# Combining the early deformable samples inside the attention and storing only their combination

## The chip, the cores and the metric

The program runs on one core of a Trainium2 chip. A core has five engines that run side by side, each with its own in-order stream of instructions: TensorE (PE, with its weight loads PEld), VectorE (DVE), ScalarE (ACT), GpSimd (POOL) and SyncE (SP). They tell each other by semaphores when a tile is ready or free. DMAs are issued from the streams of SP, POOL and ACT and run on 16 DMA engines. SBUF is the on-chip memory with 128 partitions, PSUM the small accumulator memory that PE writes. The metric is the device time of one execution in microseconds (us); the median of several runs is given.

## The reference, cut to what matters

The input has two images of 256 channels and 64 x 64 pixels, all in fp32. Four layers follow each other:

1. group norm, attention with 4 heads over all 4096 pixels, projection, residual;
2. a position term is added;
3. a bottleneck: 1x1 convolution to 64 channels, a modulated deformable 3x3 convolution, 1x1 convolution back, residual;
4. two deformable 3x3 convolutions over 256 channels, each after a group norm and a ReLU, and a residual.

The deformable convolution of layer 4 samples the image at nine displaced positions per pixel, each from four neighbours:

```python
y0, x0 = jnp.floor(py), jnp.floor(px)
wy1, wx1 = py - y0, px - x0
out = (gather(y0, x0) * (wy0 * wx0) + gather(y0, x0 + 1) * (wy0 * wx1)
     + gather(y0 + 1, x0) * (wy1 * wx0) + gather(y0 + 1, x0 + 1) * (wy1 * wx1))
...
out = jnp.einsum('bckhw,ock->bohw', sampled, w.reshape(O, C, KK))
```

With separate weights for the two axes, the left pair of neighbours (both rows) can be scaled by wx0, the right pair scaled by wx1 and added, and the two rows of the result then weighted by wy0 and wy1.

## The kernel before, in words

**Two phases.** `attention` computes layer 1 for both images, and in the gaps of its loop the bottleneck of image 0 and the preparation of layer 4 for image 0. `deform` then computes the four deformable convolutions (two images, two layers) and, in the gaps of its first part, the bottleneck of image 1. The order of PE, ACT, DVE and POOL is the order in which the program emits the instructions; SP's is placed by the framework.

**The attention loop.** It runs over score tiles n of 128 queries by 1024 keys, 256 for each of four units (image, pair of heads), two tiles per turn of the loop; such a turn is called a pair here. A pair evicts the transposes of tile n-1, computes the scores of n+2 and n+3 on PE (L583), their row maxima on DVE (`lowest`, L595) and exponentials on ACT (`exponentials`, L601), transposes the exponentials of n and n+1 on PE (`turn`, L613), copies the transposes out of PSUM (`keep`, L630 on DVE and L632 on ACT) and multiplies those of an earlier tile with the values (`attend`, L642). A finished product is copied by DVE (L474). Steps with a due time (`own`) and background generators (`back`) are worked off at fixed places of the pair: `small(n)`, `small(n + 1)` and `background`. Among the due steps are the sharing of the softmax sums through DRAM (`spread`: SP stores shares, waits, and loads f), the weighting on POOL (`combine`, L522 to L530, at steps that are multiples of 16 plus 4) and the projection (`project`, L547).

**The early samples.** In the last unit the generator `early_samples` works out, for the first EARLY = 5 blocks of 512 pixels of image 0, where to sample (`offsets`, `corners`), and puts 36 samples per block in a queue: nine taps times four groups of 128 pixels, 180 samples in all. `self.sample()` is called at the end of every pair, twice, or once where n % 16 == 4. A call can store one gathered sample to DRAM and gather one: the gather (L858, POOL) fetches for each of 128 pixels one row of `img3`, which holds upper and lower neighbour side by side, and its right neighbour: 4 x 256 values per pixel, 512 KB. The store (L1299, POOL) writes these 512 KB to `samp_d`. Three tiles hold samples under way, five once the last block's offsets are done.

**The deformable phase.** It runs over samples s: 36 per block of 512 pixels, 8 blocks per layer. Per step it issues a gather for s+8, `left(s + 3)` on ACT (L1510: the left half times its weight), `right(s + 2)` on DVE (L1516: the right half times its weight, added), `first` on ACT (L1525) and `others` on DVE (L1529 or L1535) for the two rows, transposes on PE (L1547), an eviction on ACT (L1556) and products on PE (L1566). For the 180 early samples the gather is replaced by a load from `samp_d` (L1487), the first eight issued by POOL and the others by SP. Ten tiles hold samples. In these first steps the generator `second` runs the bottleneck of image 1 (`conv`): 288 gathers on POOL (L858), weighting and adding on DVE (L1077, L1088), transposes and products on PE (L1113, L1125, L1147) that share one PSUM bank, evicted by ACT (L1117).

Of the kernel before, what the change touches and what calls it, by code (L numbers as in the profile page):

```python
# [11 lines left out]
F32 = mybir.dt.float32  # L12
# [8 lines left out]
P = 128  # L21
# [3 lines left out]
CM = 64  # L25
# [39 lines left out]
class Net:  # L65
    def __init__(self, ctx, tc, a, out):
        self.tc, self.nc, self.a, self.out = tc, tc.nc, a, out
        nc = self.nc
        const = ctx.enter_context(tc.tile_pool(name="const", bufs=1))
        self.small = ctx.enter_context(tc.tile_pool(name="small", bufs=2))  # L70
        dram = ctx.enter_context(tc.tile_pool(name="dram", bufs=1, space=DRAM))

        self.ident = const.tile([P, P], F32, name="ident")
        make_identity(nc, self.ident)
        self.vec = const.tile([P, V_COLS], F32, name="vec")
        nc.sync.dma_start(self.vec, a["vec"])
        self.sel = const.tile([P, 32], F32, name="sel")
        self.shift = const.tile([P, DWK, 32], F32, name="shift")
        self.later = [(self.sel, a["sel"]), (self.shift, a["shift"])]

        self.img2, self.img3, self.x2d = [], [], []

        self.xn_d, self.xa_d = [], []
        for b in range(B):
            self.img2.append(dram.tile([GH * GW, 2 * CM], F32, name=f"img2_{b}"))
            self.img3.append(dram.tile([GH * GW, 2 * C], F32, name=f"img3_{b}"))
            self.x2d.append(dram.tile([C, HW], F32, name=f"x2d_{b}"))
            self.xn_d.append(dram.tile([C, HW], F32, name=f"xn_{b}"))
            self.xa_d.append(dram.tile([C, HW], F32, name=f"xa_{b}"))

        self.pos_d = dram.tile([C, HW], F32, name="pos_d")

        self.samp_d = [dram.tile([4 * K2 * P, 4 * C], F32, name=f"samp_d{i}") for i in range(EARLY)]
        self.sample = lambda: False
        self.early = {}
        self.share_d = [dram.tile([16, P], F32, name=f"share_d{n}") for n in range(2)]

        vec = self.vec
        self.bn_s = const.tile([P, 4], F32, name="bn_s")
        self.bn_t = const.tile([P, 4], F32, name="bn_t")  # L100
# [80 lines left out]
    def attention(self, bott):  # L181
# [5 lines left out]
        with ExitStack() as ctx:  # L187
# [492 lines left out]
            while n < last + 4 or back or more or any(own.values()):  # L680
                u, d = divmod(n, per_unit)
                if d == 0 and u < len(units):
                    plan_unit(u)
                    if u == 0:
                        back.append(prepare(1))
                    if u == 1:
                        back.append(bott.before(0, bt, ps))
                    if u == 2:
                        back.append(first_batch())
                    if u == 3:  # L690
                        back.insert(0, bott.before(1, bt, ps))
                        back.append(self.early_samples(bott, bt, held, xp, vp, kp, ps))

                def small(at):
                    steps = own.pop(at, ())
                    for f in steps:
                        f()
                    if not steps and u > 1:
                        background(1)

                if n - 1 in pts:
                    p = pts.pop(n - 1)
                    keep(n - 1, p, "ACT")
# [12 lines left out]

                small(n)
                if 4 <= n < last + 4:
                    attend(n - 4)
                    attend(n - 3)  # L720
                small(n + 1)
                if n < last:
                    pts[n + 1] = turn(e.pop(n + 1))
                if sc:
                    e[n + 3] = exponentials(n + 3, sc[1])
                if u or n % 8 == 0:
                    background(1 + (u > 1 and n % 4 == 0))

                for _ in range(2 - (n % 16 == 4)):
                    more = self.sample()  # L730
                n += 2


# [522 lines left out]
    def early_samples(self, bott, pools, held, xp, vp, kp, ps):  # L1256
# [32 lines left out]
            self.filters(wf[cb], cb, dw, pw)  # L1289
            yield True  # L1290
        free, more = deque(x.rearrange("p u n -> p (u n)") for x in xbs), [border, t]
        gathers, stores = deque(), deque()

        def gather():


            if len(stores) > 1 and len(free) < 3 or not gathers and stores:
                dst, four = stores.popleft()
                nc.gpsimd.dma_start(dst, four)  # L1299
                free.append(four)  # L1300
            if gathers:
                dst, idx = gathers.popleft()
                four = free.popleft()
                self.gather(four, self.img3[0], idx)
                stores.append((dst, four))
            return gathers or stores

        self.sample = gather
        for i in range(EARLY):
            idx = bott.corner.tile([P, 4, K2], I32, name="bidx")  # L1310
            w = bott.corner.tile([P, 4, K2, 4], F32, name="bw4").rearrange("p a k c -> p (a k c)")
            w = self.early[i] = w.rearrange("p (s j k t) -> p s j k t", s=2, j=4, t=2)
            steps = self.offsets(
                i, xs,
                lambda s, row: wf[s][:, DWK * row : DWK * row + DWK, :].rearrange(
                    "p t o -> p (t o)"
                ),
                self.vec[:, V_PWB : V_PWB + 1],
                bott.base, idx, None, pools["work"], wide, ps,
                odp=lambda: pools["t"].tile([P, 512], F32, name="bst"), y0=rows(i)[0],  # L1320
                later=ps.later, w=w,
            )
            mine = False
            for done in steps:
                if done == "bank":
                    continue
                while bott.lock and not mine:
                    yield False
                bott.lock = mine = True
                yield True  # L1330
            bott.lock = False
            if i + 1 < EARLY:
                load(i + 1)
            if i + 1 == EARLY:
                free.extend(more)
            for m in range(4 * K2):
                k, j = divmod(m, 4)
                gathers.append((self.samp_d[i][m * P : m * P + P, :], idx[:, j, k : k + 1]))

    def deform(self, bott):  # L1340

# [4 lines left out]
        with ExitStack() as ctx:  # L1346
# [130 lines left out]
            def gather(s):  # L1477
                if s < ALL:
# [4 lines left out]
                    if n == 0 and i < EARLY:  # L1483

                        queue = nc.gpsimd if s < AHEAD else nc.sync
                        m = 4 * k + j
                        queue.dma_start(four, self.samp_d[i][m * P : m * P + P, :])  # L1487
                        return
                    idx = corners[b, l, i][0]
                    self.gather(four, self.img3[b], idx[:, j, k : k + 1])  # L1490
# [6 lines left out]
            def paired(s):  # L1497
                n, i, _, j = parts(s)
                return s < ALL and (n == 0 or j % 2 == 1)

            def share(s, side, axis):
                n, i, k, j = parts(s)
                w = corners[(*layers[n], i)][2]
                return w[:, side, j, k, axis : axis + 1]

            def left(s):

                if paired(s):
                    uv = fours[s][:, 0:2].rearrange("p s c -> p (s c)")
                    nc.scalar.mul(uv, uv, share(s, 0, 1))  # L1510

            def right(s):
                if paired(s):
                    four = fours[s].rearrange("p s c -> p (s c)")
                    uv = four[:, : 2 * C]
                    nc.vector.scalar_tensor_tensor(  # L1516
# [263 lines left out]
```

## Time and profile before

| what | value |
|---|---|
| median of 3 runs | 5226.75 us (5212.4 to 5232.05) |
| profiled execution | 5197.2 us |
| its span, first to last instruction | 5195.3 us |
| PE busy | 4853.1 us (93%) |
| DVE busy | 3970.8 us (76%) |
| ACT busy | 3283.0 us (63%) |
| POOL busy | 2448.6 us (47%) |
| mean granted TensorE clock | 0.975 |
| DMA, whole execution | 1113.50 MB, mean 214 GB/s |
| samples of the early blocks stored, each 512 KB | L1299, 2416.2 to 3062.1 us |
| samples loaded back, each 512 KB | L1487, 3083.7 to 3590.8 us |

How to read it: the engines run side by side, so busy shares do not add up, and a mean over the whole execution says little about a stage. Matmuls are pipelined and their ends are modelled, so a busy PE is not PE at its peak. In a group or timeline line, the engine and line of the kernel come first, then operation, output tile, input tiles and shapes; what stands in brackets or behind the second bar is the idle time of that engine just before, with what ended it ("issue" where the profile shows no reason). Line numbers are those of the kernel before.

### The profile page before, as it was taken

What the parts mean: (1) busy time and instruction counts of PE and PEld (TensorE: products, weight loads), DVE (VectorE), ACT (ScalarE), POOL (GpSimd) and SP (SyncE); (2) the same over time, 40 slices, a digit from 0 to 9 for tenths busy, and PEclk for the clock granted to TensorE, in tenths of its full rate; (3) what the DMA queues carried; (4) which work ended last, traced back from release to release, by engine and by line L of the source; (5) the groups of instructions that cost most, each with busy time, mean ns of one, the idle gap of its engine ahead of it and who ended that gap; (6) DMA issues with size and microseconds to landing.
All of it is one profiled execution on the core that took longest, in us unless ns stands there. A gap on an engine that the chain in (4) does not pass through costs nothing.

```text
span 5195.3 us, 101328 instructions
## 1 busy us (share of the span) xinstructions
PE 4853.1 (93%) x38680; PEld 2726.4 (52%) x38680; DVE 3970.8 (76%) x7081; ACT 3283.0 (63%) x5941; POOL 2448.6 (47%) x2436
## 2 busy tenths in 40 slices
PE   8999999999999999999999976788999999999998
PEld 5555565555555555555555544444444444444443
DVE  6878767878668878765577657787778888888887
ACT  5676656666566666654566655556866766666665
POOL 0111111111117888721455557774766666666665
PEclk9999999999999999999999988889999999999999
DMA  4221111111112333326799988887989999999998
GB/s 169 64 95 52 47 56 48 42 38 38 54 56 87 117 99 111 109 89 213 261 348 355 353 327 294 293 305 283 347 326 329 367 350 352 347 394 351 354 355 299
DMA packets 398998, 1113.50 MB, mean 214 GB/s; under 512 B 65053, under 2 KB 102491, under 8 KB 398511
## 3 DMA queue, kind: packets, MB, share of 16 engines
q0 software_dynamic: 222480, 784.79, 41.7%
q1 hardware_dynamic: 175486, 322.11, 18.7%
q8 instruction: 303, 4.96, 0.4%
q14 instruction: 185, 1.51, 0.1%
q10 hardware_dynamic: 544, 0.13, 0.0%
HBM read 914.48 MB, written 183.97 MB: 211 GB/s over the span
## 4 chain that ended last, share of the span: by engine, by line
PE 27%; DMA 9%; DVE 8%; issue 5%; ACT 3%; POOL 2%; another core or an unknown queue 2%; SPq 0%; DVEq 0%; ACTq 0%; POOLq 0%
PE out L1566 12%; PE pd L815 5%; PE pt L1547 3%; DMA samp_d<-bx 2%; DVE smp L1535 2%; DMA samp_d<-xb 2%; DVE four L1516 2%; DMA four<-img,didx 2%; DVE smp L1529 1%; PE av L642 1%; DMA xb<-img,bidx 1%; PE sc L583 1%; PE pm L815 1%; DMA bx<-img,bidx 1%
## 5 line engine op out<-in xcount | busy, mean ns | idle before, releaser
L601 ACT ACTIVATE e<-sc,low 128x1024 f32<-128x1024 f32 x1024 | 1147.2, 1120 | 755.5 <-DVE low L595 715.1
L595 DVE TENSOR_REDUCE low<-sc 128x1 f32<-128x1024 f32 x1024 | 1204.6, 1217 | 272.3 <-PE sc L583 259.9
L858 POOL DMA_INDIRECT four<-img,didx x972 | 1033.9, 1064 | 582.6 <-issue 223.0
L1566 PE MATMUL out<-st,wc 128*128 128x512 f32 x2304 | 1223.3, 613 | 88.2 <-ACT st L1556 48.0
L583 PE MATMUL sc<-k,qs 64*128 64x512 f32 x2048 | 1003.7, 609 | 0.3 <-DVE k L368 0.3
L642 PE MATMUL av<-et,v 128*64 128x256 f32 x8192 | 998.1, 386 | 0.7 <-DVE et L630 0.7
L583 PE MATMUL sc<-k,q 64*128 64x512 f32 x2048 | 985.9, 608 | 0.0
L613 PEld LDWEIGHTS tt<-ident,e 64*128 64x128 f32 x16384 | 652.1, 139 | 552.1 <-issue 266.9
L632 ACT COPY et<-tt 128x512 f32<-128x512 f32 x1152 | 659.4, 585 | 205.3 <-PE tt L613 161.3
L613 PE MATMUL tt<-ident,e 64*128 64x64 f32 x16384 | 727.7, 227 | 60.8 <-ACT et L632 36.2
L630 DVE COPY et<-tt 128x512 f32<-128x512 f32 x896 | 611.9, 683 | 172.8 <-PE tt L613 164.5
L642 PEld LDWEIGHTS av<-et,v 128*64 128x64 f32 x8192 | 553.9, 137 | 308.7 <-issue 56.6
L858 POOL DMA_INDIRECT bfour<-img,bidx x576 | 611.4, 1062 | 208.8 <-issue 107.3
L1535 DVE SCALAR_TENSOR_TENSOR smp<-four,dw,smp 128x256 f32<-128x256 f32 x1296 | 625.9, 483 | 57.6 <-issue 20.8
L1547 PEld LDWEIGHTS pt<-ident,smp 128*128 128x128 f32 x2304 | 328.7, 143 | 650.1 <-issue 532.5
L522 POOL TENSOR_TENSOR o<-o,f 128x1024 f32<-128x1024 f32 x48 | 113.9, 2373 | 1086.7 <-DVE o L474 540.0
L1566 PEld LDWEIGHTS out<-st,wc 128*128 128x128 f32 x2304 | 385.2, 195 | 325.6 <-issue 212.9
L1516 DVE SCALAR_TENSOR_TENSOR four<-four,dwt 128x512 f32<-128x512 f32 x540 | 403.7, 748 | 155.7 <-ACT four L1510 116.0
L1547 PE MATMUL pt<-ident,smp 128*128 128x128 f32 x2304 | 447.9, 277 | 22.0 <-DVE smp L1529 17.2
L1510 ACT ACTIVATE four<-four,dwt 128x512 f32<-128x512 f32 x540 | 388.1, 719 | 125.1 <-DMA four<-img,didx 105.6
L583 PEld LDWEIGHTS sc<-k,qs 64*128 64x128 f32 x2048 | 348.0, 189 | 214.0 <-issue 125.8
L1556 ACT COPY st<-pt 128x1024 f32<-128x1024 f32 x288 | 289.5, 1005 | 252.1 <-PE pt L1547 175.3
(201 smaller groups left out, 5411.8 us busy)
## 6 DMA issues: line engine op xcount, KB each, us to landing
four<-samp_d SPq DMA_DIRECT2D x172, 512.0 KB
samp_d<-xb POOLq DMA_DIRECT2D x118, 512.0 KB
f<-share_d SPq DMA_DIRECT2D x128, 256.0 KB
xb<-xn SPq DMA_DIRECT2D x55, 512.0 KB
img<-imgt SPq DMA_DIRECT2D x96, 256.0 KB
xa<-res SPq DMA_DIRECT2D x32, 512.0 KB
samp_d<-k POOLq DMA_DIRECT2D x31, 512.0 KB
samp_d<-bx POOLq DMA_DIRECT2D x31, 512.0 KB
```

The source lines that it names most:

```text
L583: nc.tensor.matmul(s[:, j, :], lhsT=q[u, i // 2][int(h != j)][halves[j], at : at + P], rhs=k[u][c][halves[j], h, :], start=True, stop=True,)
L595: nc.vector.tensor_reduce(low, s, AX.X, ALU.max, negate=True)
L601: nc.scalar.activation(e.rearrange("p j n -> p (j n)"), s, AF.Exp, bias=blk.low[:, g, c : c + 1], accum_out=blk.sum[:, g, c : c + 1],)
L613: nc.tensor.transpose(pt[:, m, :], e[half, m // 4, m % 4 * P : m % 4 * P + P], self.ident[half, half],)
L630: nc.vector.tensor_copy(dst, pt)
L632: nc.scalar.copy(dst, pt)
L642: nc.tensor.matmul(now["av"][halves[h], :], lhsT=v[u][c][:, m, halves[h]], rhs=ets[j][:, m, h, :], start=(m == 0), stop=(m == 7),)
L858: self.nc.gpsimd.indirect_dma_start(out=dst, out_offset=None, in_=img, in_offset=bass.IndirectOffsetOnAxis(ap=idx, axis=0),)
L1516: nc.vector.scalar_tensor_tensor(uv, four[:, 2 * C :], share(s, 1, 1), uv, ALU.mult, ALU.add)
L1535: nc.vector.scalar_tensor_tensor(smps[s], four[:, c], weight(s, c), smps[s], ALU.mult, ALU.add)
L1547: nc.tensor.transpose(pts[u][:, c, j * P : (j + 1) * P], smp[:, c * P : c * P + P], self.ident,)
L1566: nc.tensor.matmul(outs[ob], lhsT=wc[k][:, c, ob * P : ob * P + P], rhs=sts[u][:, c, :], start=(k == 0 and c == 0), stop=(k == K2 - 1 and ...
```

## The change

The left and right halves of an early sample are combined in the attention, and only the combination, 2 x 256 values per pixel or 256 KB, is stored. `sample` becomes a line of four stations, one step each per call: SP stores a finished combination; DVE adds the weighted right half (and frees the gathered tile); ACT scales the left half of a gathered sample into a tile of the bottleneck's pool "g" (five buffers); POOL gathers the next sample. ACT takes a sample only when all tiles but one hold gathered samples, or when there is nothing left to gather. One of the two calls per pair moves from the end of the pair to behind `small(n)`, before the products. In the deformable phase the load fetches 256 KB, and `left` and `right` skip the early samples (`whole`); `first` and `others` do what they did.

```diff
-        self.samp_d = [dram.tile([4 * K2 * P, 4 * C], F32, name=f"samp_d{i}") for i in range(EARLY)]
+        self.samp_d = [dram.tile([4 * K2 * P, 2 * C], F32, name=f"samp_d{i}") for i in range(EARLY)]
...
                 small(n)
+                if n % 16 != 4:
+                    self.sample()
                 if 4 <= n < last + 4:
...
-                for _ in range(2 - (n % 16 == 4)):
-                    more = self.sample()
+                more = self.sample()
                 n += 2
...
-        gathers, stores = deque(), deque()
-
-        def gather():
-
-
-            if len(stores) > 1 and len(free) < 3 or not gathers and stores:
-                dst, four = stores.popleft()
-                nc.gpsimd.dma_start(dst, four)
+        gathers, landing, scaled, stores = deque(), deque(), deque(), deque()
+        tiles = len(free)
+
+        def sample():
+
+            if stores:
+                nc.sync.dma_start(*stores.popleft())
+            if scaled:
+                dst, four, uv, w = scaled.popleft()
+                nc.vector.scalar_tensor_tensor(
+                    uv, four[:, 2 * C :], w[:, 1], uv, ALU.mult, ALU.add
+                )
                 free.append(four)
-            if gathers:
-                dst, idx = gathers.popleft()
+                stores.append((dst, uv))
+            if len(landing) >= tiles - 1 or not gathers and landing:
+                dst, four, w = landing.popleft()
+                uv = pools["g"].tile([P, 2, 4, CM], F32, name="bfour")
+                uv = uv.rearrange("p k s c -> p (k s c)")
+                nc.scalar.mul(uv, four[:, : 2 * C], w[:, 0])
+                scaled.append((dst, four, uv, w))
+            if gathers and free:
+                dst, idx, w = gathers.popleft()
                 four = free.popleft()
                 self.gather(four, self.img3[0], idx)
-                stores.append((dst, four))
-            return gathers or stores
+                landing.append((dst, four, w))
+            return gathers or landing or scaled or stores
...
             if i + 1 == EARLY:
                 free.extend(more)
+                tiles += len(more)
...
-                        queue.dma_start(four, self.samp_d[i][m * P : m * P + P, :])
+                        queue.dma_start(four[:, : 2 * C], self.samp_d[i][m * P : m * P + P, :])
...
+            def whole(s):
+                n, i, _, _ = parts(s)
+                return paired(s) and (n > 0 or i >= EARLY)
...
             def left(s):
 
-                if paired(s):
+                if whole(s):
...
             def right(s):
-                if paired(s):
+                if whole(s):
```

More of the change, by code (lines that the diff above doesn't have):

```diff
@@ L1291, in early_samples @@
         free, more = deque(x.rearrange("p u n -> p (u n)") for x in xbs), [border, t]
-        gathers, stores = deque(), deque()
-        def gather():
-            if len(stores) > 1 and len(free) < 3 or not gathers and stores:
-                dst, four = stores.popleft()
-                nc.gpsimd.dma_start(dst, four)
-                free.append(four)
-            if gathers:
-                dst, idx = gathers.popleft()
+        gathers, landing, scaled, stores = deque(), deque(), deque(), deque()
[8 more added lines that the diff above has]
+                )
+                free.append(four)
+                stores.append((dst, uv))
[7 more added lines that the diff above has]
+                dst, idx, w = gathers.popleft()
                 four = free.popleft()
                 self.gather(four, self.img3[0], idx)
-                stores.append((dst, four))
-            return gathers or stores
-        self.sample = gather
+                landing.append((dst, four, w))
+            return gathers or landing or scaled or stores
+        self.sample = sample
         for i in range(EARLY):
@@ L1335, in early_samples @@
                 free.extend(more)
+                tiles += len(more)
             for m in range(4 * K2):
                 k, j = divmod(m, 4)
-                gathers.append((self.samp_d[i][m * P : m * P + P, :], idx[:, j, k : k + 1]))
+                gathers.append(
+                    (self.samp_d[i][m * P : m * P + P, :], idx[:, j, k : k + 1], w[:, :, j, k, 1:2])
+                )
     def deform(self, bott):
```

## The prediction

> **What bounds the kernel now.** I read the page's slices first, then a table of stretches, then single engines inside the two stretches that the change touches.
>
> The slices (tenths of busy time in 130 us each) show TensorE (PE) full except in slices 25 to 29, where the granted clock falls too:
>
> ```profile
> PE   8999999999999999999999976788999999999998
> ...
> PEclk9999999999999999999999988889999999999999
> DMA  4221111111112333326799988887989999999998
> ```
>
> The early samples are gathered in the attention's last quarter and loaded back in the first part of the deformable stage. Busy time of PE, its weight loads, DVE, ACT and POOL there, then clock, DMA share, GB/s:
>
> ```profile
> 2411.00:3062.00 651.00, 622.19 (x6251) 360.19 (x6249) 422.66 (x687) 396.29 (x741) 328.31 (x395) 0.98 0.90 322
> 3083.00:3592.00 509.00, 378.29 (x1597) 220.59 (x1598) 377.68 (x761) 266.00 (x463) 341.83 (x313) 0.83 0.83 289
> 3592.00:5195.00 1603.00, 1507.27 (x5446) 744.76 (x5444) 1328.01 (x2950) 1077.01 (x1900) 1033.90 (x972) 0.99 0.95 349
> ```
>
> In the attention PE is 96% busy, DVE 65%, ACT 61%. In the second stretch no engine is full: PE 74% at clock 0.83. The third is untouched.
>
> The order of one attention pair (two score tiles) decides what DVE and ACT have to spare, so I read the timeline of two pairs without side work, first DVE, then ACT:
>
> ```profile
> 2814.86 2.36 DVE L595 TENSOR_REDUCE low<-sc 128x1 f32<-128x1024 f32 x2 [0.20 <-PE sc L583]
> 2817.13 0.68 DVE L630 COPY et<-tt 128x512 f32<-128x512 f32 x1
> 2819.66 2.36 DVE L595 TENSOR_REDUCE low<-sc 128x1 f32<-128x1024 f32 x2 [1.85 <-PE sc L583]
> 2821.93 0.68 DVE L630 COPY et<-tt 128x512 f32<-128x512 f32 x1
> 2822.88 0.42 DVE L474 COPY o<-av 128x256 f32<-128x256 f32 x1 [0.27 <-PE av L642]
> 2823.75 0.69 DVE L630 COPY et<-tt 128x512 f32<-128x512 f32 x1 [0.44 <-PE tt L613]
> 2824.47 2.35 DVE L595 TENSOR_REDUCE low<-sc 128x1 f32<-128x1024 f32 x2
> ```
>
> ```profile
> 2817.75 1.13 ACT L601 ACTIVATE e<-sc,low 128x1024 f32<-128x1024 f32 x1
> 2818.76 0.21 ACT L601 ACTIVATION_READ_ACCUMULATOR e<-sc,low 128x1 f32 x1
> 2818.85 1.08 ACT L632 COPY et<-tt 128x512 f32<-128x512 f32 x2
> 2820.97 1.12 ACT L601 ACTIVATE e<-sc,low 128x1024 f32<-128x1024 f32 x1 [1.04 <-issue]
> ...
> 2825.79 1.11 ACT L601 ACTIVATE e<-sc,low 128x1024 f32<-128x1024 f32 x1 [1.49 <-DVE low L595]
> ```
>
> Two pairs take 9.61 us (2814.86 to 2824.47). In that time DVE idles 1.85+0.27+0.44 = 2.56 us and ACT 1.04+1.49 = 2.53 us.
>
> Last, POOL between 3092 and 3556, where it issues the second batch's 288 gathers (its group, then its waits):
>
> ```profile
> L858 POOL DMA_INDIRECT bfour<-img,bidx x288 | 326.2, 1133 | 123.4 <-issue 68.6 <-DVE bsmp L1088 28.2 <-DVE smp L1529 7.9
> ```
>
> ```profile
> POOL bfour L858 <- issue: 68.6, 225, 0.4
> POOL bfour L858 <- DVE bsmp L1088: 28.2, 10, 6.5
> POOL bfour L858 <- DVE smp L1529: 7.9, 26, 0.3
> POOL bfour L858 <- DMA x<-xn: 7.3, 2, 4.0
> ```
>
> Single gathers there come every 0.95 + 0.30 us at best, so 288 need 360 us of the 445 that they take: POOL is nearest to full, and the excess is longer instructions (326.2 - 288 x 0.95 = 53 us) and waits (123.4 - 288 x 0.30 = 37 us).
>
> **The attention: added work.** Each of 180 samples gets one ACT multiply (L1510's row: 0.72 us, following work 0.61 later) and one DVE multiply-add (L1516's: 0.75, next 0.66 later). There are 15 sample calls per 8 pairs, so they fall on 96 pairs, nearly two per pair. Over two clean pairs DVE gets 4 x 0.66 = 2.64 us against 2.56 idle, ACT 2.44 against 2.53: both become full, and part of their idle time is waiting for PE's order. I wrote the pair down in emission order, from PE's first score product, with the spacings of the rows. Now PE starts its first transposes at 1.78 and its second at 4.24, which is when three chains end together: PE's own products, and the evictions on ACT and on DVE. With the change ACT does, from its first exponential on: eviction at +1.11, multiply at +1.58, second exponential at +2.19, second multiply at +3.29, free at +3.90. In the pair that opens with one ACT eviction, the maximum on DVE slips by 0.07 and so do the first exponential (2.52) and the end: 4.86 us for 4.79. Its second multiply then ends at 6.42, which is 1.56 into the next pair. That one opens with two ACT evictions (0.96), and PE's first transposes, which need the PSUM buffers, start at 2.74 instead of 1.78: 5.75 us. Its own second multiply ends 0.67 into the pair after, which is early enough. Together 10.61 for 9.58, or 0.51 per pair. From PE's timeline, 62 of the 105 pairs between 2405 and 3066 us are shorter than 5.4 us, so about 57 of 96: 57 x 0.51 = 29 us. Longer pairs have PE side work to hide behind, except where DVE or ACT is busy as well: the pair 2881.32 to 2886.51 has DVE at 4.98 of 5.19 us, the one from 2865.75 ACT at 4.59 of 4.84. Two such in 16 pairs at 1 us each: 12 us. Sum **+41**. Its ends: 0, if all hides beside PE, and 180 x 0.66 = +119, if DVE's share is wholly exposed; I take the worked schedule, since it returns 4.79 for the pair as it is. A gain from added instructions is excluded.
>
> **New waits in the attention.** ACT's multiply waits for its gather, with exponentials queued behind it and PE behind those. In the chain of waits a gather takes 6.4 to 8.0 us from issue to landing. With 5 tiles it is used four calls later, 9.6 us in clean pairs; with 3 tiles (first 37 samples, to about 2545 us) only two calls, some 5 to 6 us, though several of those pairs last 20 us. POOL's next gather waits for DVE to free the tile. The 180 stores move from POOL to SP: each issue costs 0.32 us on a queue with room, but stands behind SP's wait for the shares to land (57.3 us in 14 waits), and the ring of five result buffers leaves three calls for a store to land. No row shows these waits. Each is bounded by 0 and about 24 us: 2 us (8.0 against 6) on some 12 early samples, and 2 us (4.1 of SP's wait, less what three calls leave over) on 12 share steps. Of 0 to 48 I take **+8**, near the lower end, because most budgets exceed the landing rows and the stores are half as long as those shown.
>
> **What is moved.** One of the two sample calls moves ahead of the products: on POOL it passes nothing, since the combination steps (L522 to L528) fall on even steps and the call after them is still left out; its ACT and DVE parts are in the schedule above.
>
> **What the attention gets back.** POOL loses 180 store issues and the waits around them (samp_d<-xb 79.1 us alone); on PE's path only its wait for POOL's avs counts, 10.2 us in two places: **-10** (0 to -12). Stores of half the size also free DMA time (share 0.90), which bounds nothing else there.
>
> **The deformable stage.** Removed: 180 ACT multiplies (125 us busy) and 180 DVE multiply-adds (129 us) between 3083 and 3592, and half of every load. ACT at 52% and loads that ACT waits 2.1 us for are credited with nothing: POOL, PE and DVE work covers them. I credit POOL's excess. Longer gathers: DVE's instructions that read two SBUF tensors take 129 (L1516), 81 (L1529), 98 (L1077) and 61 us (L1088) there; the first goes, and I take its share of the 53 us, 53 x 129 / 369 = 19 us. Of 37 us of waits, 28.2 are for bsmp on DVE, which falls from 74% to 49%: 22 us. At the start PE stands 16.3 us for the first gather behind some 10 full-size loads; halving these takes 2.6 MB away, 9 us at 289 GB/s, of which I take 6 since weights queue there as well. **-47**. Ends: 0, if PE's halts remain for other reasons, and -(445 - 360) - 9 = -94.
>
> The row says that gathers of 966 ns in the attention become 1133 beside these multiply-adds. The Trainium skill's page SBUF — State Buffer, section Who interferes with whom, says that a VectorE instruction with two SBUF inputs collides with GpSimd's reads, but infers that descriptor generation needs the write interface; by it the 19 us would be 0, and the net +11 rather than -8. I keep the row.
>
> **Sum.** +41 + 8 - 10 - 47 = -8 us. The profiled execution took 5197.2 us (span 5195.3 and 1.9 around it), 29.6 under the median of 5226.75; it would become 5189, the median **5219**. What can be told from no change is 0.5%, 26 us.
>
> **Rivals.** *Attention becomes ACT/DVE bound (slower).* In front of the exponential and of the evictions, a delay passes to PE whole. For it: the three chains that end together at 4.24 us. Against: 34 pairs have side work. At 1.2 us for each of 96 pairs it is +115 + 8 - 10 - 47 = +66, 5293; it ends slower than before from (47 + 2)/96 = 0.51 us per pair, and past 0.5% from 0.78; the forecast has 41/96 = 0.43. *Hidden in the attention, full gain after (faster).* If PE's order absorbs all but 12 us and POOL comes within 5 us of its 360: 12 + 8 - 10 - 80 - 6 = -76, 5151. For it: the mean pair is 6.3 us, where DVE's 65% would become 86%. Against: the clean pairs. *The deformable stretch does not move.* PE halts of 7 to 11 us there (3162, 3268, 3384) end in "issue" or in ACT waiting for PE, with no cause shown; if these set the pace, -15 instead of -47 gives +24, 5251. That the work is done twice is excluded: `whole` keeps these samples out of left and right.
>
> **Chances.** Forecast 0.34, faster rival 0.30, slower rival 0.24, unmoved stretch 0.12. The forecast's own range is 5195 to 5245, and a fifth of it lies past -26 us; half of the last rival lies past +26. Faster: 0.30 + 0.07 = 0.37; slower: 0.24 + 0.06 = 0.30; within: 0.33. The range, 5140 to 5295, takes in both outer rivals and about half of what lies around them.
>
> **What would show it.** Right: clean pairs at 4.9 and 5.7 us in turn; the stretch from the last attention product to the first didx gather near 450 us, bfour gathers near 1.05 us, clock above 0.83, no POOL wait for samp_d. Wrong: ACT's multiply waiting for "xb<-img,bidx" over 50 us in sum, pairs of 6 us, or PE's halts at L1113 as many as now.

## The result, and the profile after

The kernel after takes 5265.2 us (median of 7 runs) against 5226.75 us before: a ratio of 1.0073, 95% interval 1.0054 to 1.0092, 38 us slower where 8 us less had been forecast. A second comparison, in another session, gave 1.0071 (1.0052 to 1.0090). The profiled execution took 5267.2 us, span 5265.4; the one of the kernel before, 5197.2, lies 30 us under its own median.

The slices of the page of the kernel after (PE, its granted clock, DMA; 132 us each) have much the same dent as before, in slices 24 to 27, though DMA is down:

```profile
PE   8999999999999999989999986779999999999998
...
PEclk9999999999999999999999988889999999999999
DMA  5221111111113333345688865667999999999998
```

The table of stretches of the kernel after (busy time of PE, its weight loads, DVE, ACT and POOL; then clock, DMA share, GB/s). The second stretch begins later than before's, since the attention ends later:

```profile
2411.00:3062.00 651.00, 616.57 (x5892) 335.45 (x5894) 513.16 (x829) 479.16 (x877) 229.74 (x215) 0.99 0.77 250
3120.00:3592.00 472.00, 335.72 (x1391) 196.85 (x1394) 234.42 (x512) 137.09 (x256) 296.70 (x300) 0.81 0.64 196
...
3592.00:5195.00 1603.00, 1505.58 (x5474) 748.33 (x5468) 1302.92 (x2911) 1049.32 (x1860) 1012.07 (x952) 0.98 0.93 342
```

All the work that was to go did go. In the attention DVE has 90 and ACT 83 us more, in the second stretch DVE is at 50% and ACT at 29%, and the DMA share fell from 0.83 to 0.64. Only the time did not follow. Measured by PE's transposes of the first and the 181st sample, the early stretch took 514.8 us before and 529.3 after. The attention's last quarter, from the scores of tile 812 to those of tile 1020, went from 655.1 to 691.9 us, +36.8.

Two clean pairs of the kernel after, DVE first, then ACT (start, duration, and in brackets idle time before):

```profile
2851.16 0.74 DVE L1302 SCALAR_TENSOR_TENSOR bfour<-bx,bw,bfour 128x512 f32<-128x512 f32 x1
2851.95 0.75 DVE L1302 SCALAR_TENSOR_TENSOR bfour<-xb,bw,bfour 128x512 f32<-128x512 f32 x1
2853.05 2.41 DVE L595 TENSOR_REDUCE low<-sc 128x1 f32<-128x1024 f32 x2 [0.35 <-PE sc L583]
...
2857.27 0.42 DVE L474 COPY o<-av 128x256 f32<-128x256 f32 x1 [0.54 <-PE av L642]
```

```profile
2851.18 0.73 ACT L1311 ACTIVATE bfour<-xb,bw 128x512 f32<-128x512 f32 x1
2851.81 1.11 ACT L601 ACTIVATE e<-sc,low 128x1024 f32<-128x1024 f32 x1
...
2852.90 0.72 ACT L1311 ACTIVATE bfour<-xb,bw 128x512 f32<-128x512 f32 x1
2853.51 1.07 ACT L632 COPY et<-tt 128x512 f32<-128x512 f32 x2
```

The starts of their first score products on PE are 2847.07, 2851.93, 2857.70, 2862.62 and 2868.42: pairs of 4.86, 5.77, 4.92 and 5.80 us, which is the forecast's 4.86 and 5.75 in turn.

Now the second stretch. POOL's group and the longest waits of the kernel after, 3130 to 3600 us (in a wait: us in total, times, longest):

```profile
L859 POOL DMA_INDIRECT bfour<-img,bidx x284 | 289.0, 1018 | 176.2 <-DVE bsmp L1089 83.5 <-issue 76.0 <-DMA four<-samp_d 11.3
```

```profile
ACT bst L1118 <- remote: 123.8, 11, 20.4
DVE smp L1548 <- ACT smp L1544: 118.5, 23, 9.7
...
POOL bfour L859 <- DVE bsmp L1089: 83.5, 23, 7.1
...
PE pm L1114 <- issue: 41.4, 9, 15.6
```

The gathers became shorter, 1018 for 1133 ns, as forecast. But POOL's waits for DVE's `bsmp` went from 28.2 to 83.5 us instead of going away. DVE waits for ACT's `smp`, and ACT waits in front of an eviction for something that the profile cannot name. One such halt in the order of time (kernel after, all engines):

```profile
3208.53 1.95 PE L1114 MATMUL pm<-ident,bsmp 128*128 128x128 f32 x16
...
3211.36 0.91 ACT L1544 ACTIVATE smp<-four,bw 128x256 f32<-128x256 f32 x2
...
3213.56 0.38 PE L1566 MATMUL pt<-ident,smp 128*128 128x128 f32 x2
...
3217.60 0.95 POOL L859 DMA_INDIRECT bfour<-img,bidx  x1 [0.30 <-issue]
3218.32 0.42 DVE L1089 TENSOR_TENSOR bsmp<-bfour 128x256 f32<-128x256 f32 x1 [4.59 <-remote]
3218.85 0.94 POOL L859 DMA_INDIRECT bfour<-img,bidx  x1 [0.30 <-issue]
...
3226.35 0.94 POOL L859 DMA_INDIRECT bfour<-img,bidx  x1 [0.30 <-issue]
3228.91 0.58 ACT L1118 COPY bst<-pm 128x512 f32<-128x512 f32 x1 [16.64 <-remote]
3229.55 2.82 PE L1114 MATMUL pm<-ident,bsmp 128*64 128x128 f32 x12 [15.61 <-issue]
```

PE's transposes of L1114 are recorded as done at 3210.5, ACT is done with its earlier work at 3212.3 and PE's last recorded matmul ends at 3213.9, yet the eviction of L1118 starts at 3228.91. From 3213.9 on only POOL works, but for one addition of DVE: one gather every 1.25 us without a break, until POOL runs out of buffers at 3227.3.

The trace also holds times at which PE raised its semaphore, that is, reported a product as ready. Not every raise is in it (162 of 202 between 3150 and 3550 us, kernel after). Those that are, matched in order to the latest matmuls that can have made them, come up to 0.05 us after the recorded end in 95 of 100 cases through the first 1500 us. In this halt the four pairs of transposes recorded up to 3210.5 report at 3218.29, 3220.44, 3223.26 and 3228.89, and the eviction starts 0.02 us after the last. So PE reports up to 18 us late, and its records hide it. I call this PE's lag. The raises of DVE and ACT in these 400 us come within 0.03 us of their recorded ends, so the lag is PE's alone. Whether PE's products are late or only its reports, the trace does not tell; who waits for them loses the time either way.

Between 3150 and 3550 us, 95 of 100 of PE's raises lag by less than 14.2 us before and 13.1 after. In the kernel after, where gathers in a run start 1.33 us apart on average, a lag of over 1 us begins 6 to 16 us into a run and is as a rule over within 4 us of its end. In the kernel before they start 1.45 us apart, in runs of up to 80; there the lag begins only 28 to 45 us into a long run, and in two of them PE catches up in between.

### The profile page after: what moved, and what is told of

Read it like the earlier page. It is cut to its first block, busy times and chain, and to the rows that moved or that the text cites. A ratio compares the mean times of both kernels' runs of the same rounds, so it can differ in the third digit from the quotient of the medians.

```text
span 5265.4 us, 101951 instructions
## 1 busy us (share of the span) xinstructions
PE 4897.2 (93%) x38680; PEld 2728.6 (52%) x38680; DVE 3965.8 (75%) x7081; ACT 3271.8 (62%) x5941; POOL 2314.2 (44%) x2256
## 4 chain that ended last, share of the span: by engine, by line
PE 33%; DVE 9%; ACT 5%; issue 4%; another core or an unknown queue 3%; DMA 2%; POOL 0%; SPq 0%; DVEq 0%; ACTq 0%; POOLq 0%
PE out L1585 14%; PE pd L816 5%; PE pt L1566 4%; PE av L642 2%; DVE low L595 2%; DVE smp L1554 2%; PE sc L583 1%; PE tt L613 1%; PE pm L1114 1%; PE pm L816 1%; DVE four L1535 1%; DVE bfour L1302 1%; ACT smp L1544 1%; ACT e L601 1%
## 5 line engine op out<-in xcount | busy, mean ns | idle before, releaser
L613 PE MATMUL tt<-ident,e 64*128 64x64 f32 x16384 | 745.9, 227 | 68.9 <-ACT et L632 42.8
L859 POOL DMA_INDIRECT bfour<-img,bidx x576 | 575.2, 999 | 263.0 <-issue 116.9
```

What stands on the lines that cost most here:

```text
L613: nc.tensor.transpose(pt[:, m, :], e[half, m // 4, m % 4 * P : m % 4 * P + P], self.ident[half, half],)
L859: self.nc.gpsimd.indirect_dma_start(out=dst, out_offset=None, in_=img, in_offset=bass.IndirectOffsetOnAxis(ap=idx, axis=0),)
```

## The experiments

The theory after reading the two traces: PE falls behind while POOL issues gathers in close order, and this sets the length of the early stretch. Rivals: the deformable gain was real and the attention cost twice as much ("the gain was eaten"); PE's transposes, evictions and transposes again halt each other through the one PSUM bank; the DMA traffic does it. "Stretch" below is the first to the 181st sample's transposes in the profiled execution.

**Each part of the change alone.** e1 is the deformable part on the kernel before:

```diff
-                        queue.dma_start(four, self.samp_d[i][m * P : m * P + P, :])
+                        queue.dma_start(four[:, : 2 * C], self.samp_d[i][m * P : m * P + P, : 2 * C])
...
             def left(s):
-                if paired(s):
+                if whole(s):
```

> The deformable part of the change alone, on the kernel before: the attention stores full samples as it did, the loads fetch only the first 256 KB of each, and left and right skip the early samples (so the right halves of these samples are left out of the result). Theory 'PE is starved by runs of gathers': TensorE falls behind its own records whenever POOL issues gathers back to back, and this sets the length of the stretch; less work on DVE and ACT and half the load bytes change nothing, so the time is that of the kernel before within 12 us and the stretch stays between 500 and 530 us. Rival 'the gain was eaten' (my forecast's step was right and the attention cost more than the trace says): 47 us faster than the kernel before, the stretch near 468 us.

Measured: 5198.8 us against 5199.6, ratio 0.9997 (0.9984 to 1.0009); the stretch is 511.4 us. The step that I had priced at -47 is worth nothing. POOL's group of this run, 3092 to 3556 us, shows how:

```profile
L858 POOL DMA_INDIRECT bfour<-img,bidx x288 | 296.1, 1028 | 159.9 <-issue 76.4 <-DVE bsmp L1088 64.6 <-DMA four<-samp_d 10.6
```

Without DVE's multiply-adds, ACT's multiplies and half the loaded bytes the gathers are 30 us shorter in sum (326.2 to 296.1), and POOL's idle time is 36.5 us longer (123.4 to 159.9). From the first gather's start to the last one's end it is 445.5 us before and 445.3 here.

e2 is the attention part alone:

```diff
-                        queue.dma_start(four[:, : 2 * C], self.samp_d[i][m * P : m * P + P, :])
+                        src = self.samp_d[i][m * P : m * P + P, :].unsqueeze(1).to_broadcast([P, 2, 2 * C])
+                        queue.dma_start(four.rearrange("p (t n) -> p t n", t=2), src)
...
             def whole(s):
-                return paired(s) and (n > 0 or i >= EARLY)
+                return paired(s)
```

> The attention part of the change alone, on the kernel after: the combined sample is stored, but the deformable phase loads it twice (512 KB again) and runs left and right on it for the early samples (so these samples are weighted a second time). Theory 'starved by runs of gathers': the attention alone costs the whole difference, +30 to +45 us over the kernel before, level with the kernel after within 12 us. Rival 'the gain was eaten': the deformable work comes back on top, +80 to +90 us over the kernel before.

Measured: 5239.9 us, ratio 1.0080 (1.0059 to 1.0101), +40 us, the whole difference. Putting 180 multiplies, 180 multiply-adds and 47 MB of loads back costs nothing: the stretch is 510.2 us. The rival "the gain was eaten" is out.

**The gathers of the second bottleneck as plain loads.** e3 changes the kernel after, e7 does the same on POOL's queue, e8 does it to the kernel before:

```diff
+                        dst = fours[n][:, m].rearrange("p s c -> p (s c)")
+                        if b:
+                            at = 2 * P * ((4 * i + j) % 16)
+                            src = net.img2[b][at : at + 2 * P, :]
+                            nc.sync.dma_start(dst, src.rearrange("(p r) c -> p (r c)", r=2))
+                            continue
```

> The kernel after with the 288 gathers of the second bottleneck (128 rows of 1 KB each) replaced by plain loads of the same size and row shape, issued by SP from fixed rows (so this bottleneck samples at fixed places). The bytes, the PSUM bank and the work of DVE, ACT and PE stay. Theory 'starved by runs of gathers': PE's completions follow its records within 2 us, the halts of 5 to 20 us go, the stretch falls from 529 to 400-460 us and the time by 70 to 130 us below the kernel after. Rival 'one PSUM bank' (transposes, eviction and transposes again share one bank and halt each other) and rival 'DMA traffic': the halts stay, the stretch stays above 510 us and the time within 20 us of the kernel after.

Measured: 5092.4 us, ratio 0.9797 (0.9776 to 0.9818), 148 us below e2 on the same chip. The stretch is 358.5 us, PE's lag in it nowhere above 0.1 us. Its row in the table of stretches, and what its evictions wait for:

```profile
3120.00:3497.00 377.00, 356.50 (x1681) 207.75 (x1682) 276.63 (x621) 173.46 (x318) 28.10 (x37) 0.95 0.87 293
```

```profile
ACT bst L1124 <- PE pm L1120: 81.7, 39, 4.2
```

PE is busy 95% of the time at clock 0.95, beside a DMA share of 0.87, higher than in the kernel after. The PSUM bank is the same. Both these rivals, the one bank and the DMA traffic, are out: it is the gathers.

> As the run with plain loads instead of the second bottleneck's gathers, but issued by POOL instead of SP (this bottleneck again samples at fixed places). Theory 'it is the gathers' row-by-row lists of addresses': plain loads need none, PE keeps up and the time is within 25 us of the run with SP's plain loads. Rival 'it is whatever POOL issues': PE falls behind as with the gathers, and the time is over 5170 us.

Measured: 5103.8 us, ratio 0.9764 (0.9745 to 0.9784); stretch 364.4 us, lag in it at most 0.1 us. Plain loads that POOL issues do PE no harm here; the gathers do.

> The kernel before with the second bottleneck's gathers as plain loads on SP (fixed places). With PE no longer starved, does the work that the change takes from DVE and ACT count? If it does (my forecast's step, valid once POOL's gathers are gone): DVE's 378 us of work set the pace, the stretch is 400 to 430 us against 358 in the kernel after with plain loads, and the time is level with that one (5080 to 5110 us, the attention's 40 given back). If it does not: the stretch is 355 to 370 us and the time 40 us below the kernel after with plain loads, near 5050 us.

Measured: 5126.3 us, ratio 0.9815 (0.9788 to 0.9843), on the chip of e7; the stretch is 431.0 us, and PE does not lag (0.1 us at most). So once PE is not held up, the change takes 67 to 72 us out of the stretch (431.0 to 364.4 in e7, or to 358.5 in e3, which like e8 loads from SP's queue but ran on another chip). After the attention's 37 a gain is left: 22 us against e7 (5126.3 to 5103.8), 9 us against e3 by the ratios. The forecast's step comes true, in a program that is not this one.

**Pauses between the gathers.** e4 was to shorten the runs through fewer buffers:

```diff
-            second = bott.conv(1, bott.pools(inner, 8, 7), ps)
+            second = bott.conv(1, bott.pools(inner, 4, 7), ps)
```

> The kernel after with 4 instead of 8 buffers for the second bottleneck's gathers, so that POOL can issue at most 8 gathers ahead before it has to wait for DVE, instead of 16; nothing is left out. Theory 'starved by runs of gathers': runs of 20 to 30 gathers become runs of 10 or so, TensorE falls at most some 5 us behind instead of 18, the stretch shortens by 20 to 60 us and the time with it. Rivals 'one PSUM bank' and 'DMA traffic': fewer buffers only take look-ahead away, so 0 to +30 us.

Measured: 5236.0 us, ratio 1.0080 (1.0054 to 1.0107), level with e2, so no shift; the stretch is 504.6 us in the profiled execution, the fastest of four. The edit did not do what it was for: DVE freed buffers while POOL went on, runs of 18 to 24 gathers remained, and the lag reached 16.1 us. It tells nothing against either side. e5 puts pauses in by hand:

```diff
+                    if b and n % 3 == 2:
+                        for _ in range(3):
+                            nc.gpsimd.memset(self.pause, 0.0)
...
+            bott.pause = wp.tile([P, 512], F32, name="pause")
             second = bott.conv(1, bott.pools(inner, 8, 7), ps)
```

> The kernel after; after every 6 gathers of the second bottleneck POOL clears a scratch tile three times (about 0.53 us each, 1.6 us together, by the row of a 128x512 clear). Nothing is left out. Theory 'starved by runs of gathers': in the kernel after PE kept up through the first 7 or so gathers of a run and then fell behind, so with a pause after every 6 it stays within 4 us of its records, the stretch falls from about 510-530 to 440-490 us and the time by 40 to 90 us below the kernel after. Rival 'any busy POOL starves PE': the clears are no pause, the halts stay, and 48 x 1.6 = 77 us of POOL time lengthen the stretch by 30 to 80 us.

Measured: 5253.2 us, ratio 1.0051 (1.0034 to 1.0068), some 11 us below the kernel after by the ratios, where 40 to 90 had been expected; stretch 515.4 us. PE kept up (95% of the lags under 1.75 us, none over 3.6), as expected, but the time was given to POOL: its six gathers and the pause take 9.5 us, 456 us in all. e6 and e9 change only the pattern, two clears after every two gathers and one after every four:

> The same with two clears (1.1 us) after every 2 gathers. POOL then needs 144 x (2 x 1.25 + 1.1) = 518 us for this bottleneck whatever PE does. Theory 'starved by runs of gathers': PE stays within 2 us of its records and has no halts without a cause, but POOL now sets the pace: the stretch is 510 to 550 us, level with the kernel after within 25 us. Rival 'any busy POOL starves PE': PE falls behind by 10 us and more as before, on top of POOL's longer time: a stretch over 570 us.

Measured: 5315.7 us, ratio 1.0170 (1.0149 to 1.0190); some 50 us above the kernel after by the ratios and a stretch of 584.2 us, both longer than I expected. PE's lag is at most 0.1 us with the same gathers and a busier POOL, so it is neither POOL's work as such nor the number of gathers, but how closely they follow each other. The waits of e6, 3130 to 3700 us, now name engines that do wait for each other: DVE waits for the gathers, so POOL's pace sets the length:

```profile
DVE bfour L1081 <- DMA bfour<-img,bidx: 261.4, 128, 9.4
ACT bst L1121 <- PE pm L1117: 249.8, 35, 19.8
```

> The kernel after with one clear (0.53 us) after every 4 gathers of the second bottleneck; nothing is left out. With three clears per six gathers PE kept up, but POOL itself then needed 48 x 9.5 = 456 us. With one clear per four POOL needs 72 x (4 x 1.25 + 0.65) = 407 us. Theory 'starved by runs of gathers', with a short pause being enough: PE falls behind by at most 5 us, the stretch is 440 to 480 us, the time 35 to 75 us below the kernel after. Rival 'PE bears some 1.6 us per gather and no less, whatever the pattern': PE falls behind by 8 us and more again, the stretch stays at 500 to 530 us and the time within 15 us of the kernel after.

Measured: 5216.7 us, ratio 1.0034 (1.0020 to 1.0049), 20 us below the kernel after by the ratios; stretch 492.7 us. The shorter pause costs POOL less, but PE still falls behind by up to 18 us in places. Neither expectation was met in full. With the same pause in the kernel before (e10):

> The kernel before with the same single clear after every 4 gathers of the second bottleneck. Its gathers take 1.43 us each, so POOL needs 72 x (4 x 1.43 + 0.65) = 459 us. Theory 'a short pause is enough': PE at most 5 us behind, the stretch 465 to 495 us for about 515, the time 20 to 45 us below the kernel before. Rival '1.6 us per gather': within 15 us of the kernel before.

Measured: 5188.0 us, ratio 0.9977 (0.9962 to 0.9992); stretch 510.0 us, 95% of the lags under 5.6 us. It is the fastest version here that computes everything, by 10 us or 0.2%, less than the 20 to 45 us expected.

Spread over all 288, a gather took 1.48 us in e9, 1.53 in e10, 1.59 in e5 and 1.82 in e6, and the greatest lags were 18, 12, 3.6 and 0.1 us. So a bound on the gathers per time that PE bears, the rival named for e9, fits as well as the lack of breaks; these runs do not tell the two apart.

**The attention's two engines.** e11 moves the multiply to POOL, e12 and e13 leave out ACT's or DVE's instruction:

```diff
-                nc.scalar.mul(uv, four[:, : 2 * C], w[:, 0])
+                nc.gpsimd.tensor_scalar_mul(uv, four[:, : 2 * C], w[:, 0])
```

> The kernel after with the early samples' multiply in the attention moved from ACT to POOL, which is idle for over half of that time; nothing is left out. If the attention's 37 to 40 us come from ACT's multiply standing before the exponential and the evictions (the forecast's schedule, 0.51 to 0.74 us for each of 96 pairs), 20 to 35 us of them go. If they come from DVE's multiply-add, the time stays within 10 us of the kernel after. If POOL's slower multiply holds up its own combination steps, the time rises.

Measured: 5265.5 us, ratio 1.0120 (1.0098 to 1.0142). The attention's last quarter grew to 726.7 us:

```profile
2411.00:3062.00 651.00, 578.22 (x5626) 330.37 (x5624) 512.40 (x795) 354.27 (x663) 517.32 (x368) 0.98 0.72 235
```

POOL has 517 us of work for 230, about 1.6 us per multiply, and PE is down to 578 us. The new bound hides what I wanted to know.

```diff
-                    uv, four[:, 2 * C :], w[:, 1], uv, ALU.mult, ALU.add
+                    uv, four[:, 2 * C :], w[:, 1], four[:, : 2 * C], ALU.mult, ALU.add
...
-                nc.scalar.mul(uv, four[:, : 2 * C], w[:, 0])
```

> The kernel after with ACT's multiply of the early samples in the attention left out: DVE adds the weighted right half to the unweighted left half. If the pairs are longer because ACT's multiply stands before the exponential and the evictions (the forecast's schedule), 25 to 40 us go and the time is level with the kernel before within 12 us. If it is DVE's multiply-add, the time stays within 10 us of the kernel after. If either engine alone can hold a pair, 10 to 20 us go.

```diff
-                nc.vector.scalar_tensor_tensor(
-                    uv, four[:, 2 * C :], w[:, 1], uv, ALU.mult, ALU.add
-                )
                 free.append(four)
```

> The kernel after with DVE's multiply-add of the early samples in the attention left out: the weighted left half alone is stored. If ACT's multiply makes the pairs longer (the forecast's schedule), the time stays within 10 us of the kernel after. If it is DVE's multiply-add, 25 to 40 us go. If either engine alone can hold a pair, 10 to 20 us go.

Measured: 5053.1 us and 5063.2 us, ratios 0.9946 (0.9929 to 0.9962) and 0.9959 (0.9947 to 0.9972). On this chip the kernel before took 5082.2 us, 116 to 148 us below the other sessions, so the expectations, stated as times, cannot be judged by the times. The last quarter of the attention took 661.4 and 669.7 us; on the other chips every kernel with before's attention took 653.8 to 656.9 and all but one with after's 691.9 to 693.6 (the other 688.8; e11, with its own attention, aside). So without ACT's multiply some 6 us of the 37 remain, without DVE's multiply-add some 15. Of the kernel before there is no trace on this chip, and code that is alike runs a little faster on it: the scores of tiles 100 to 700 took 1687 us against 1694 to 1698, those of 500 to 700 607 against 614 to 618. By these shares, 0.5 and 1.4%, before's last quarter would be 3 to 9 us shorter here, and the 6 and 15 become 9 to 15 and 18 to 24, an estimate. Either way more than a third of the 37 goes when one of the two instructions is left out, so neither engine alone makes the pairs that long.

This chip also showed something else. POOL's group of e12, 3090 to 3500 us:

```profile
L859 POOL DMA_INDIRECT bfour<-img,bidx x288 | 293.3, 1019 | 98.7 <-issue 60.6 <-DMA bfour<-img,bidx 14.3 <-DMA four<-samp_d 11.6
```

No wait for `bsmp` is among its main ones: all 288 gathers go through in one unbroken run of 381 us, and PE does not lag (0.1 us at most, in the later stage too, where on the other chips it does). The stretch is 438.5 us, the later stage, from the 181st sample's transposes to the last, 1505 us against 1562 to 1589. PE's lag under runs of gathers was thus seen on three of the four chips that the experiments ran on (numbers 2, 0 and 15 on record; the fourth is 12), not on all; whether it is the chip or something else of that one session is not shown.

The traces differ in one thing more. Between 3150 and 3550 us that of the kernel after holds 521 of the 854 raises that PE, DVE and ACT made, that of e12 1081 of 1082, that of e3 1264 of 1345, that of e6, where PE keeps up, 628 of 780. Every execution on record has a granted clock beside its time, so each seems to have been recorded in this way. That the recording has a part in PE's halts is a rival that no run here excludes.

Of e12's -29 us against before the attention's +6 is a part, so the deformable part is worth about -35 there; e13 gives -19 - 15 = -34 (with the larger remainders above, up to -44 and -43). To measure that directly I ran the kernel after and e1 once more, and got a chip of the other kind:

> The kernel after, unchanged. On a chip where PE is held up by runs of gathers (many short runs of gathers in the trace, the stretch over 500 us): 1.005 to 1.010 of the kernel before, as already measured. On a chip where it is not (one unbroken run of 288 gathers, the stretch near 440 us): the attention's +37 and the deformable part's -35 cancel, within 0.3% of the kernel before.

> The deformable part alone on the kernel before (the right halves of the early samples left out), again. On a chip where PE is held up by runs of gathers: within 0.2% of the kernel before, as already measured. On a chip where it is not: 25 to 50 us faster, because the second bottleneck's gathers then set the pace and are shorter without DVE's multiply-adds.

Measured: ratios 1.0071 (1.0052 to 1.0090) and 0.9993 (0.9982 to 1.0005), with stretches of 519.9 and 521.7 us and 95% of the lags under 14 us. Both came out as expected for a chip where PE is held up. The -35 us stay an estimate by difference.

## Why the prediction was wrong

**The attention: +41 + 8 - 10 = +39.** Right in sum: its last quarter grew by 36.8 us in the first two profiles (32 to 40 over all the chips that lag), with clean pairs of 4.9 and 5.8 us in turn. The three terms were not measured one by one. For the added work, that both engines are full is borne out by e12 and e13, though I had let ACT's second multiply carry it alone. The new waits, +8, look too high: ACT waits 3.8 us in all for gathers to land, in four places. Of the -10, PE's 10.2 us of waiting for POOL's `avs` are gone from its waits in the loop, while its waits for ACT's evictions rose from 4.9 to 13.7 us.

**The deformable stage, -47.** This step failed: e1 measured -1 us (-8 to +5). I had counted 53 us of longer gathers and 37 us of POOL's waits as POOL's own excess over 360 us, and credited 19 and 22 of them. The first did shrink, by 30. The second was not POOL's own and grew by as much: as the halt shows, its waits for `bsmp` on DVE were PE's lateness, handed on from PE to ACT's eviction, from there to `first` and `others`, and from DVE to POOL's free buffers. With shorter gathers POOL only reaches the next such wait sooner. What the forecast missed is that POOL is not free to run at its own pace: gathers in close order hold up PE (e3, e6, e7). The six for the first loads were not seen either: in e1 the first transposes start at 3102.6, before at 3103.4.

**The rival "the deformable stretch does not move"** was what happened; it gave 5251 us, 14 below the result, and I held it at 0.12. The halts with no cause shown that speak for it were in the profile, and a wait by "issue" or "remote" on every engine at once deserved more than a remark.

**What would have shown it.** Clean pairs and shorter gathers came as written. The stretch, the clock (0.81) and the halts at PE's conv transposes came as the signs against.

**The two profiled executions** differ by 70 us, the medians by 38. The attention and the early stretch account for 48 of the 70; in the rest the later stage is 21.6 us longer after (1567.7 to 1589.3 us from the 181st sample's transposes to the last). Kernels that are alike there spread from 1562 to 1589 us on the chips of this kind, so I put that down to the executions and not to the change.

The page that I weighed, SBUF — State Buffer, section Who interferes with whom, infers that a two-input VectorE instruction leaves GpSimd's descriptor generation alone. For gathers the row was right to be kept: in e1 those beside no work of DVE take 0.95 us (94 of them), those beside nothing but the two-input L1077 1.13 us (11). Plain loads issued by POOL, in e7, take 0.54 us with or without L1077 beside them (17 and 21 of them), which fits the page. A gather also reads its row numbers (`bidx`) from SBUF; whether that is where it waits no run here shows. The same section of the Trainium skill says that PE waits on no other engine at SBUF; through what POOL's gathers hold up PE no run here shows, but that they do, by 18 us in the halt shown, follows from e3 and e6, save for the open rival of the recording.

## What to carry to other kernels

Before a wait is credited to the engine that it names, follow it to the first engine that is late, and compare the times of that engine's semaphore with its recorded ends: here the named releasers were two and three steps behind the cause. Where several engines halt together and the profile gives no reason, relief for any one of them should be priced at zero until a run with that stage changed says otherwise; leaving out one part (e1, e2) would have answered it at once. Gathers that POOL issues in close order can slow PE, so they are better spread over stages with room, or set apart where POOL has time to spare: a short pause after every four gained 0.4% and 0.2% here (e9, e10), a long one after every two cost 1% (e6).

## What the hardware showed that I had not expected

- On three of four chips PE's reports of finished products fall behind its recorded matmuls, by up to 18 us in the halt shown and by under 14.2 us in 95 of 100 cases, while POOL issues indirect gathers in close order: from 6 to 16 us into a run with one every 1.33 us, from 28 to 45 us with one every 1.45. Plain loads of the same bytes, from SP or POOL, leave it under 0.1 us, and so does a pause of 1.1 us after every two gathers. The way in which it acts, and whether the recording of the traces has a part in it, is open.
- In the one session on the fourth it did not show: 288 gathers in 381 us without a break, lag under 0.1 us, and the kernel before at 5082 us instead of 5198 to 5230.
- In such a halt the recorded end of a matmul does not tell when others can use its result: the eviction shown starts 18 us after it. The granted clock fell to 0.5 at 3218.6 in the halt shown, when the first of the four reports had already come 9 us late (3218.29 for a recorded end at 3209.1), so the clock did not start it.
- A gather on POOL takes 0.95 us undisturbed and 1.13 us beside a VectorE multiply of two SBUF tensors; a plain load issued by POOL takes 0.54 us in both cases.
